# Layer 0 of a graph network in rounds of two pairs of batches (256 moving columns), with the mask's identity product taken from TensorE

## The chip, the cores and the metric

The kernel runs on one core of one Trainium2 chip. The metric is the device time of one execution in microseconds (us); a kernel is compared with the kernel before in rounds on the same chip. All times below are medians of several executions; a profile shows one execution, and its span is some 2 us shorter than the measured time.

## The reference

Four layers work on `x` (32 batches, 512 nodes, 128 features, float32) with one 512 x 512 matrix `adj`. Every layer adds a function of `h = relu(layernorm(x))` to `x`:

```python
# layer 0: an attention matrix A from the mask adj > 0 (the same for all batches)
m = adj > 0
vals = e[0][cumsum(m) - 1]
A = softmax(where(m, vals, NEG), axis=1)
x += (A * I) @ (h @ W[0]) + (A * (1 - I)) @ (h @ W[1]) + bias
# layer 1: hops with adj and its Chebyshev square, products with Theta, relu
# layer 2: weights = adj * adj; messages = weights^T @ relu(h @ psi); two small products
# layer 3: attention of h with itself, masked by adj
```

Layer 0 multiplies the same 512 x 512 matrix with the projected `h` of all batches. Layer 2 needs `adj` once more, in another order of its rows; the kernel reloads it (1 MB, called `sq`) and squares it at about 300 us.

## The kernel before

Batches go in pairs (16 of them). Layer 0 handles one pair in each round: a projection `g` of `h`, then seven half-size products instead of eight, each of 2 x 2 matmuls that move 128 columns, into three accumulators `a`, `c`, `d`, then terms for the diagonal.

```python
ORDER = ((1, "a", True), (6, "c", True), (5, "d", True), (7, "c", False), (2, "a", False),
         (4, "c", False), (3, "d", False))
def by_token(p, a, b, first):
    for i in range(2):
        for k in range(2):
            nc.tensor.matmul(p[:, i * D : (i + 1) * D], a[:, k, blk(i)], b[:, k, :], ...)
# [cut]
def project_steps(q, hT):
    g[q] = pair_tile(f"g_{q}")...            # five buffers of 2 x 512
    pg = [projected(f"p_g_{q}_{b}", (at(hT, b), w0[:, 1, :])) for b in range(2)]
```

`hT` is `h` with features on the partitions. From the fourth pair on it is made by VectorE (32 x 32 blocks) and a bounce through DRAM: four writes `d_hT` (128 KB each) and one read `hT` (512 KB), issued by SyncE, whose instructions follow one another in every trace here.

```python
d = bounce.tile(...)
for i in range(NQR):
    nc.sync.dma_start(d[:, :, i, :]..., hb[i * QR : (i + 1) * QR]...)
hT = feature_major(name)
nc.sync.dma_start(hT..., d...)
```

Square matrices share four buffers of 1 MB. `sq` is allocated in the code of layer 1, but its load is placed by a scheduler.

```python
def square_tile(name):
    return const.tile([P, NT, N], F32, tag="square", name=name, bufs=4)
# in the order of allocation: adj_s, cheb, att, attT, then sq (in att's place), adjTx, ...
def square():
    sq = square_tile("sq")
    load_crossed(sq, adj)                    # four transfers of 256 KB, by SyncE
    adjTx.append(square_tile("adjTx"))
    load_crossed(adjTx[0], adjT_d)
```

## Time and profile before

| | before |
|---|---|
| time, median of 3 (range) | 977.85 us (976.84 to 979.55) |
| span of the profile | 976.0 us |
| first product of layer 0 | 38.29 us |
| third pair's first product (the first two pairs done) | 63.89 us |
| first product of layer 1 | 200.2 us |
| layer 1's first product to the end | 775.8 us |

### The profile page before, as it was taken

What the parts mean: (1) busy time and instruction counts of PE and PEld (TensorE: products, weight loads), DVE (VectorE), ACT (ScalarE), POOL (GpSimd) and SP (SyncE); (2) the same over time, 40 slices, a digit from 0 to 9 for tenths busy, and PEclk for the clock granted to TensorE, in tenths of its full rate; (3) what the DMA queues carried; (4) which work ended last, traced back from release to release, by engine and by line L of the source; (5) the groups of instructions that cost most, each with busy time, mean ns of one, the idle gap of its engine ahead of it and who ended that gap; (6) DMA issues with size and microseconds to landing.
All of it is one profiled execution on the core that took longest, in us unless ns stands there. A gap on an engine that the chain in (4) does not pass through costs nothing.

```text
span 976.0 us, 16214 instructions
## 1 busy us (share of the span) xinstructions
PE 965.5 (99%) x5925; PEld 802.1 (82%) x5926; DVE 596.1 (61%) x1420; ACT 467.5 (48%) x1057; POOL 411.3 (42%) x519
## 2 busy tenths in 40 slices
PE   8999999999999999999999999999999999999998
PEld 4889999999999999999977777777667777777776
DVE  8788887755565655656576666556655444444444
ACT  3865445222322323238676644545674455444553
POOL 5779999841316313121244443344142332223322
PEclk9999999999999999999999999999999999999999
DMA  9255553522121221234343333332222121121111
GB/s 259 92 150 146 159 137 102 152 86 67 44 72 58 64 67 44 82 92 121 96 125 114 110 94 99 87 87 67 72 70 74 44 76 55 55 76 44 55 33 44
DMA packets 83056, 87.17 MB, mean 89 GB/s; under 512 B 6817, under 2 KB 73121, under 8 KB 82977
## 3 DMA queue, kind: packets, MB, share of 16 engines
q1 hardware_dynamic: 82976, 86.14, 31.1%
q8 instruction: 47, 0.77, 0.3%
q14 instruction: 33, 0.26, 0.1%
HBM read 44.70 MB, written 41.42 MB: 88 GB/s over the span
## 4 chain that ended last, share of the span: by engine, by line
PE 90%; DVE 3%; POOL 3%; ACT 1%; issue 1%; DMA 1%; DVEq 0%; POOLq 0%; ACTq 0%
PE p_av L887 12%; PE p_l L372 11%; PE p_score L872 11%; PE p_msgT_c L319 4%; PE p_x2T_c L319 4%; PE p_x1T_c L319 4%; PE p_l_c L326 4%; PE p_feat L372 3%; PE p_x1T_a L319 3%; PE p_hv L372 3%; PE p_x1T_d L319 3%; PE p_x2T_d L319 3%; PE p_x2T_a L319 3%; PE p_msgT_d L319 3%; PE p_msgT_a L319 3%; PE p_qkh L859 3%
## 5 line engine op out<-in xcount | busy, mean ns | idle before, releaser
L225 ACT ACTIVATE h<-x,sh,rs 128x128 f32<-128x128 f32 x448 | 182.5, 483 | 74.0 <-PE p_x2T_d L319 43.9
L877 POOL TENSOR_TENSOR ex<-ex,adjTx 128x512 f32<-128x512 f32 x64 | 83.4, 1305 | 206.3 <-ACT ex L875 201.7
L873 ACT ACTIVATE ex<-p_score 128x512 f32<-128x512 f32 x128 | 71.7, 588 | 122.7 <-issue 112.9
L887 PEld LDWEIGHTS p_av<-qkh_hv,ex 128*128 128x128 f32 x1024 | 118.4, 191 | 9.6 <-issue 7.2
L887 PE MATMUL p_av<-qkh_hv,ex 128*128 128x129 f32 x1024 | 120.3, 275 | 0.9 <-POOL ex L877 0.8
L872 PE MATMUL p_score<-qkh_hv,hT 128*128 128x512 f32 x256 | 115.2, 593 | 0.0
L259 DVE STREAM_TRANSPOSE hb_hT<-h 128x512 f32<-128x512 f32 x122 | 84.7, 699 | 21.0 <-ACT h L225 20.8
L877 DVE TENSOR_TENSOR ex<-ex,adjTx 128x512 f32<-128x512 f32 x64 | 46.0, 718 | 76.2 <-ACT ex L875 76.2
L872 PEld LDWEIGHTS p_score<-qkh_hv,hT 128*128 128x128 f32 x256 | 46.2, 190 | 46.5 <-issue 45.0
L197 DVE BATCH_NORM_STATS2 bn<-x 128x6 f32<-128x256 f32 x224 | 82.9, 418 | 1.3
L300 POOL TENSOR_TENSOR rt_h<-h 128x256 f32<-128x256 f32 x32 | 22.6, 728 | 133.4 <-PE p_x2T_c L319 133.1
L875 ACT ACTIVATE ex<-ex 128x512 f32<-128x512 f32 x128 | 76.6, 631 | 1.9
L300 POOL TENSOR_TENSOR rt_feat<-feat,feat 128x256 f32<-128x256 f32 x16 | 11.7, 729 | 126.7 <-ACT feat L828 126.7
L372 PE MATMUL p_l<-th,x2T 128*128 128x128 f32 x256 | 49.5, 275 | 0.0
L372 PE MATMUL p_l<-th,x1T 128*128 128x128 f32 x256 | 49.5, 275 | 0.0
L372 PE MATMUL p_l<-th,hs 128*128 128x128 f32 x256 | 49.5, 275 | 0.0
L372 PEld LDWEIGHTS p_hv<-vw,hT 128*128 128x128 f32 x256 | 33.6, 192 | 15.3 <-issue 8.1
L634 POOL COPY hs<-hT 128x512 f32<-128x512 f32 x32 | 19.6, 614 | 54.6 <-PE p_l L372 40.4
L636 POOL TENSOR_TENSOR hd<-hT,adiag 128x512 f32<-128x512 f32 x32 | 41.0, 1288 | 3.8 <-PE p_l_e L684 3.8
L209 ACT ACTIVATE sd<-bn,eps 128x8 f32<-128x8 f32 x60 | 17.9, 300 | 50.8 <-DVE bn L197 49.7
L345 ACT COPY x1T<-p_x1T_a 128x256 f32<-128x256 f32 x16 | 6.0, 372 | 74.1 <-PE p_x1T_a L319 74.1
L372 PEld LDWEIGHTS p_l<-th,hs 128*128 128x128 f32 x256 | 40.0, 192 | 0.8
(241 smaller groups left out, 2185.9 us busy)
## 6 DMA issues: line engine op xcount, KB each, us to landing
d_hT<-hb_hT SPq DMA_DIRECT2D x244, 128.0 KB, 2.4
hT<-d_hT SPq DMA_DIRECT2D x61, 512.0 KB, 3.6
x<-in_x_dram SPq DMA_DIRECT2D x28, 256.0 KB, 4.3
out_dram<-x SPq DMA_DIRECT2D x28, 256.0 KB, 2.3
adj_s<-in_adj_dram SPq DMA_DIRECT2D x4, 256.0 KB, 3.1
adjT_d<-adjT SPq DMA_DIRECT2D x1, 1024.0 KB
sq<-in_adj_dram SPq DMA_DIRECT2D x4, 256.0 KB
x_last<-in_x_dram SPq DMA_DIRECT2D x4, 256.0 KB
```

Of the source, the lines that this page charges most:

```text
L197: nc.vector.bn_stats(st[:, k].rearrange("p e s -> p (e s)"), xt[q][:, b, t : t + 2, :].rearrange("p t f -> p f t"))
L225: nc.scalar.activation(h[:, b, t, :], xt[q][:, b, t, :], AF.Relu, bias=shift[q][:, i : i + 1], scale=scale[q][:, i : i + 1])
L259: nc.vector.transpose(hb[:, :, b].rearrange("p j t r -> p t j r"), h[:, b].rearrange("p t (j c) -> p t j c", c=QR))
L319: nc.tensor.matmul(p[:, :H], b[:, k, :], a[:, k, :], start=(first and k == 0), stop=(k == 1), skip_group_check=True)
L326: nc.tensor.matmul(p[:, i * D : (i + 1) * D], a[:, k, blk(i)], b[:, k, :], start=(first and i == 0 and k == 0), stop=(k == 1), skip_group_ ...
L372: nc.tensor.matmul(p[:, blk(t)], hT(t), w, start=(i == 0), stop=(i == len(terms) - 1))
L636: nc.gpsimd.tensor_mul(split(s), src, split(scale))
L872: nc.tensor.matmul(ps, hT[:, t, b, :], qkh, start=True, stop=True)
L873: nc.scalar.activation(ex[:, t, :], ps, AF.Tanh, scale=1.0 / (8.0 * math.sqrt(D)))
L875: nc.scalar.activation(ex[:, t, :], ex[:, t, :], AF.Exp, scale=8.0)
L877: eng.tensor_mul(ex[:, t, :], ex[:, t, :], adjTx[0][:, t, :])
L887: nc.tensor.matmul(po[:, i, : D + 1], ex[:, t, blk(i0 + i)], hv[:, t, :], start=(t == 0), stop=(t == NT - 1))
```

## The change

The intent is to halve the number of matmuls in the products of layer 0 (two pairs share the stationary half of the attention matrix), and to take four matmuls with the identity off TensorE. A round now has two pairs, and `g` of such a round needs 1 MB. Buffers of 1 MB (`quad`, two of them) replace the pair buffers; where those don't suffice, every third `g` goes into a square buffer.

```diff
-        nc.tensor.matmul(p[:, i * D : (i + 1) * D], a[:, k, blk(i)], b[:, k, :],
+        nc.tensor.matmul(p[:, i * 2 * D : (i + 1) * 2 * D], a[:, k, blk(i)], b[:, k],
@@ [cut]
-    def pair_tile(name):
-        return work.tile([P, 2 * N + 2 * NT], F32, tag="pair", name=name, bufs=5)[:, : 2 * N]
+    def quad_tile(name):
+        return work.tile([P, 2, 2 * N + 2 * NT], F32, tag="quad", name=name, bufs=2)
@@
-        g[q] = pair_tile(f"g_{q}").rearrange("p (t b f) -> p t b f", t=NT, b=2)
+        r, w = divmod(q, 2)
+        if w == 0:
+            if r % 3 == 2:
+                g[r] = square_tile(f"g_{r}").rearrange("p t (b w f) -> p t b w f", b=2, w=2)
+            else:
+                t = quad_tile(f"g_{r}")...
@@ [cut: the start]
+    def entries(t):
+        nc.scalar.mul(us[t], m[:, t, :], elastn)
+        nc.gpsimd.tensor_add(att[:, t, :], us[t], att[:, t, :])
@@
-            nc.tensor.matmul(ph, at_row[:, kk, blk(t)], at_col[:, kk, :], start=(kk == 0), stop=False)
-        nc.tensor.matmul(ph, identh, m[:, t, :], start=False, stop=True)
+            nc.tensor.matmul(ph, at_row[:, kk, blk(t)], at_col[:, kk, :], start=(kk == 0), stop=(kk == NK - 1))
@@ [cut: rounds of two pairs, order of the start, buffers of layers 1 to 3]
```

## The prediction

> **What bounds the kernel now.** I read part 1 of the page first (which engine is full), then the chain of waits, then the windows of single rounds (what a round consists of), and last the timeline of the first 64 us, the only stretch where TensorE isn't simply full.
>
> ```profile
> PE 965.5 (99%) x5925; PEld 802.1 (82%) x5926; DVE 596.1 (61%) x1420; ACT 467.5 (48%) x1057; POOL 411.3 (42%) x519
> ```
>
> TensorE is busy 965.5 us of a span of 976.0; nothing else is above 82%. So the time is TensorE's queue of matmuls plus about 10 us in which it waits. Only two things can shorten the kernel: fewer or cheaper matmul cycles, or less of that waiting. The chain of waits shows where layers 0 and 1 lie and their periods:
>
> ```profile
> 113.43 1.79 PE p_g L372 x16
> 123.26 1.79 PE p_g L372 x16
> 133.08 1.79 PE p_g L372 x16
> ...
> 212.47 5.36 PE p_l L372 x48
> 229.91 5.36 PE p_l L372 x48
> ```
>
> Columns: start, duration, work, instructions. Layer 0 takes one pair of batches in 9.83 us (113.43 to 123.26), layer 1 in 17.44 us. A round of layer 0 is 56 product records (7 products, 4 matmuls each, every f32 matmul appearing as two records), 16 for the diagonal and 16 for p_g: 88 records in 9.825 us are 0.1117 us each, for 128 moving columns. The 48 p_l records say the same, 5.36 / 48 = 0.1117. Windows of one round of layer 0, and of the 56 product records of a layer-1 round (which move 256 columns):
>
> ```profile
> 113.43:123.26 9.83, 9.83 (x90) 9.83 (x90) 8.37 (x23) 4.76 (x12) 9.26 (x11) 1.00 0.57 163
> ...
> 217.83:229.91 12.08, 12.08 (x56) 10.28 (x55) 1.00 0.28 80
> ```
>
> In the first, PE, PEld, DVE, ACT and POOL follow the length: PE is full, GpSimd is busy 9.26 of 9.83, VectorE 8.37. In the second, 56 records of 256 columns take 12.08 us, 0.2157 each. So the width that this change brings is already measured inside this kernel. The start of layer 0 from the timeline:
>
> ```profile
> 25.30 0.70 ACT L563 ACTIVATE u<-u,least 128x512 f32<-128x512 f32 x1
> ...
> 33.87 1.04 PE L405 MATMUL p_attT<-ident,att 128*128 128x128 f32 x8
> ...
> 38.29 1.06 PE L326 MATMUL p_l_a<-g,attT 128*128 128x128 f32 x8
> ...
> 54.95 1.13 PE L326 MATMUL p_l_c<-rt_g,attT 128*128 128x128 f32 x8 [1.01 <-DVE u_l L696]
> ...
> 88.02 1.13 PE L326 MATMUL p_l_c<-rt_g,attT 128*128 128x128 f32 x8 [1.64 <-DVE u_l L696]
> ```
>
> Layer 0 starts at 38.29; layer 1's first product starts at 200.21 in the same view. The brackets are waits of TensorE for VectorE's eviction of an accumulator that is to be added to again.
>
> **What the Trainium skill says.** "TensorE: Matmul & The Clock Gate", section "Back-to-back issue gap", tabulates 134, 262 and 518 cycles for 128, 256 and 512 columns at 2.4 GHz: a fixed cost of about 6 cycles per matmul, whatever its width. Twice that (an f32 record behaves like two passes) is 111.7, 218.3 and 431.7 ns; the trace has 111.7, 215.7 and, for p_score (3.44 us for 8), 430. It agrees within 1.2%, and it says that doubling the width saves only the fixed cost, not half the time. The same section gives 81 ns for a sustained pair of weight load and 128-column matmul; no such floor shows above 111.7 ns here. "SBUF — State Buffer", section "SBUF: two separate sides", says that a VectorE instruction with two SBUF inputs and a GpSimd instruction lock one port pair against each other. The trace agrees in kind: the four sums of the attention matrix on VectorE took 742 ns for the first and 1107 to 1214 ns for those beside GpSimd's rt_g. "ScalarE: Activation LUTs", section "What ACT_TABLE_LOAD costs", gives 1283 ns and a drain of about 1380 ns; the trace has 1283 ns and the next instruction directly after it, so I count 1.28.
>
> **The change part by part.**
> (1) Products of layer 0: 16 x 56 = 896 records of 128 columns at 0.1117 become 448 of 256 at 0.2157. 100.1 us become 96.6: -3.4 us, all of it TensorE time in a stage that TensorE bounds. Diagonal and p_g records keep number and width. A round of two pairs is then 56 x 0.2157 + 64 x 0.1117 = 19.2 us where two rounds were 19.65.
> (2) The identity product on the mask: 4 matmuls of 512 bf16 columns leave (p_row, of the same form, takes 1.89 us for 8, so 0.24 each): 0.9 us of TensorE. But between 7.8 and 29.3 us VectorE runs with only one gap worth naming (0.90, before the reciprocal at 26.12) and feeds these matmuls, so I count nothing for it directly. In its place come 4 ScalarE multiplications (about 0.6 each, like the 589 ns of other 128x512 ones) and 4 GpSimd additions (1.29 each, like hd): 2.4 us and 5.2 us on engines that also make the first two normalised h. GpSimd's additions for rows 0 and 1 stand ahead of the first rs/sh chain: that chain ends at about 17.2 instead of 16.1. The second normalisation (8 x 0.40) is now wholly ahead of the first exponential, which I put at 26.8 instead of 25.30; the attention's last row leaves ScalarE at about 33.2 instead of 31.56.
> (3) Round 0 needs the projections of both first pairs. By the order of instructions, the last transposes of the attention matrix end at about 35.6 (34.9 before), and the attT copies wait on ScalarE for the square-root table (1.28) and on VectorE for g (2 x 0.69) and statistics (1.4). I get a first product at about 37.2, a little earlier than 38.29, because the Chebyshev matmuls that preceded it are moved into round 0. But after this product TensorE's queue has the transposes of pair 2, whose h ends on ScalarE at about 41: a wait of some 2.2 us. From 41.1 the rest of round 0 is 24.4 us of matmuls: 6 products 10.4, Chebyshev 6.9, diagonal 3.6, p_g 3.6. So round 1 starts at about 65.5. The kernel before had done the same work at 63.89: +1.6.
> (4) From there on, before: 136.3 us to 200.21, of which the work is 134.0 and waits are 2.3. After: 7 rounds of 19.24 less the 3.6 of p_g that the last lacks: 131.1 us, if nothing waits. That is -5.2.
> (5) VectorE: 16 evictions of 256 elements (425 ns) become 8 of 512 (about 0.69): 6.8 to 5.5 us per two pairs. GpSimd: eight rt of 0.75, six additions and two biases of 0.73 become 4 + 3 + 1 of 1.29: 11.8 to 10.3 us. Both get freer, off the path. Layers 1 to 3: the order of TensorE's instructions is the same apart from one swap of neighbours and the grouping of a few; the larger buffers keep the same depth (two pairs). I count 0.
> Sum: +1.6 - 5.2 = -3.6 us, to about 974.
>
> **The rivals.**
> Nothing but width and waits cancel: the longer start eats the gain (first exponential 2 to 3 us late, a longer wait for pair 2), giving 976 to 979. For it: the start is a chain through four engines, and two pairs now have to be ready. Against it: Chebyshev matmuls fill some of it.
> GpSimd becomes the bound of a round. For it: 9.26 of 9.83 us today, and it makes rt only after the projection of the second pair, 5.2 us of matmuls ahead of the product that needs it; ScalarE's copies take about 0.9 and two rt 2.6, so about 1.7 us are free. If sums of the adjacency matrix (1.28 each, two a round in four rounds) get in the way, each such round waits 1 to 2 us: 978 to 982. Against it: its work falls by 1.5 us per two pairs.
> The waits vanish and the start is no worse: then waits of about 4 us in layer 0 go too: about 969. For it: the accumulator that TensorE waited for at 54.95 and 88.02 was read 0.9 us of matmuls after it was written; now a product of 1.7 us, and mostly a projection of 1.8 us, stand between.
> Weight loads were the real limit of 128-column products (PEld is full in layer 0): then halving the loads would save far more. Against it: p_l in layer 1 runs at the same 0.1117 with PEld not full, and the 256-column rate is twice that within 3.5%.
>
> **Range and chances.** The sure part is -3.4; waits in layer 0 can add up to -4 more or give 4 back; the runs before spread over 2.7 us. I predict 973.8, with 969.5 to 978.0 for 8 in 10. Faster by 2% would need 958: there isn't that much waiting in the stage. Slower by 2% would need a wait of 3 us in each of the 8 new rounds.
>
> **What would show it.** The 448 products at 0.216 us each in a window of one round, and rounds of about 19.2 us from the second on (step 1, 4). The first exponential at 26 to 27.5 (step 2). The first product of layer 0 at 36 to 39 and a wait of TensorE just after it for the h of pair 2; the second round at 64 to 67 (step 3). The first product of layer 1 at about 196.6 instead of 200.21, and from there the same 776 us to the end (step 5). I am wrong if products take clearly less than 0.21, if rounds wait for rt or evictions, or if layers 1 to 3 change by more than 1 us.

## More of the kernel before

Columns: start, time until the issues were done, engine and line, what was transferred, number of issues.

```profile
35.06 2.74 SPq L99 DMA_DIRECT2D sq<-in_adj_dram  x4
...
160.61 1.76 SPq L264 DMA_DIRECT2D d_hT<-hb_hT  x4
...
164.48 0.34 SPq L267 DMA_DIRECT2D hT<-d_hT  x1
```

The reload of `adj` goes out at 35 us, in the start, between the loads of parameters and the first `hT`. In a round of layer 0 the read of `hT` follows its four writes by 3.9 us.

## The result, and the profile after

The changed kernel took 986.63 us (986.32 to 988.31, 6 executions), the kernel before 978.18 us (976.84 to 979.55) beside it. The ratio is 1.0088, 95% interval 1.0075 to 1.0101. (A ratio here is the mean time of one kernel's fast runs over that of the other's of the same rounds, so it is not quite the ratio of the medians.) So the kernel became slower by 0.9%, which counts as the same within 2%, but it lies outside the predicted range of 969.5 to 978.0.

The last two columns below belong to two experiments and are used later.

| us | before | changed | own buffers | own buffers, identity on TensorE |
|---|---|---|---|---|
| first exponential | 25.30 | 27.21 | 27.60 | 25.16 |
| second round of two pairs starts | 63.89 | 66.94 | 67.07 | 65.22 |
| first product of layer 1 | 200.2 | 209.0 | 199.1 | 197.2 |
| from there to the end | 775.8 | 775.6 | 775.6 | 775.8 |
| time, median | 978.2 | 986.63 | 976.54 | 974.58 |

Part 1 of the page of the changed kernel:

```profile
PE 965.6 (98%) x5473; PEld 788.0 (80%) x5474; DVE 597.3 (61%) x1363; ACT 469.6 (48%) x1059; POOL 402.7 (41%) x451
```

There are 452 matmul records fewer, as intended, but TensorE's busy time has not fallen at all. The table says where to look: layers 1 to 3 are unchanged, and everything is lost before layer 1. The chain of waits of the changed kernel in the last rounds of layer 0 (start, duration, work, instructions):

```profile
160.00 1.74 PE p_l_d L337 x8
161.83 0.71 SPq L99
...
163.95 10.68 DMA hT<-d_hT
...
174.76 3.76 PE p_g L385 x16
178.52 2.08 PE p_l_d L337 x8
```

Up to 163.4 the rounds take the predicted 19.24 us (the first of them 19.48). Then the chain leaves TensorE: three issues on SyncE's line 99 (the reload), one read of `hT` in flight for 10.68 us, and only then the projection `p_g` of pair 14. The projection itself takes 3.76 us, where it takes 1.79 before (shown in the prediction). TensorE waited 7.67 us for this `hT`. SyncE's queue of the changed kernel at this place:

```profile
157.57 1.75 SPq L269 DMA_DIRECT2D d_hT<-hb_hT  x4
161.83 1.88 SPq L99 DMA_DIRECT2D sq<-in_adj_dram  x3
163.95 0.39 SPq L272 DMA_DIRECT2D hT<-d_hT  x1
```

The reload, at 35 us before, now stands between the write and the read of an `hT` that TensorE wants at 167.1. The read goes out 2.4 us later than in the run with own buffers below (163.95 against 161.52), and its flight is some 7 us longer (10.68, against 3.4 in the median of this kernel). The reason is a buffer: the first free square buffer after the start is now taken by `g` of round 2 and then of round 5, and the load of `sq` has to wait for the last product of round 5 (the view of SyncE's waits has one of 2.4 us of line 99 for `p_l_d`). Windows of 2 us around the wait (length, then busy time and records of PE, PEld, DVE, ACT, POOL, granted clock, DMA share, GB/s):

```profile
172.00:174.00 2.00, 0.00 (x0) 0.00 (x0) 0.00 (x0) 0.00 (x0) 2.00 (x3) 0.57 0.48 143
...
176.00:178.00 2.00, 2.00 (x11) 2.00 (x11) 0.00 (x0) 0.58 (x1) 0.04 (x1) 0.50 0.40 89
...
180.00:182.00 2.00, 2.00 (x11) 1.76 (x10) 0.00 (x0) 0.00 (x0) 0.00 (x0) 1.00 0.06 14
```

The granted clock fell to half during the wait (at about 172) and came back only at about 179: this is why `p_g` and the `p_l_d` after it run long (3.76 + 2.08 for 1.79 + 1.73, 2.3 us). This also hides the wait in part 1: TensorE's busy time contains the slow records. "TensorE: Matmul & The Clock Gate" of the Trainium skill, section "What's actually happening", gives a clock of 4/8 after an idle window of about 3.4 us; the trace agrees, 0.50 after 7.67 us of idling, but a run below shows the same fall after shorter waits. Wait and slow clock make 10.0 us, which is the distance of 9.9 us between "changed" and "own buffers" in the table.

The second, smaller loss is in the start. The timeline of the changed kernel:

```profile
18.11 3.19 ACT L230 ACTIVATE h<-x,sh,rs 128x128 f32<-128x128 f32 x8 [2.93 <-POOL sh L212]
21.21 1.32 ACT L521 ACTIVATE u<-m,elastn 128x512 f32<-128x512 bf16 x2
...
24.11 3.19 ACT L230 ACTIVATE h<-x,sh,rs 128x128 f32<-128x128 f32 x8
27.21 0.71 ACT L594 ACTIVATE u<-u,least 128x512 f32<-128x512 f32 x1
...
42.49 1.97 PE L337 MATMUL p_l_c<-rt_g,sums_att 128*128 128x256 f32 x8 [0.81 <-DVE sums_att L290]
```

ScalarE works without a gap from 18.11 to the first exponential. It starts 2.0 us later than before (16.15), because GpSimd's chain for the first normalisation, with two of the new additions ahead of it, ends later, and two of the new multiplications (1.32 us) are among its work. The first exponential comes at 27.21, 1.9 us later than before (25.30), and the second round of two pairs starts 3.05 us later than the equal point before. (The six `at_part` on VectorE also slowed, from 2.17 to 4.08 us, beside two of GpSimd's additions. But VectorE had the first row's minimum ready at 26.19, so the exponential did not wait for them.)

### The profile page after: what moved, and what is told of

The parts are those of the page before. It is cut to its first block, busy times and chain, and to the rows that moved or that the text cites.

```text
span 984.6 us, 15193 instructions
## 1 busy us (share of the span) xinstructions
PE 965.6 (98%) x5473; PEld 788.0 (80%) x5474; DVE 597.3 (61%) x1363; ACT 469.6 (48%) x1059; POOL 402.7 (41%) x451
## 4 chain that ended last, share of the span: by engine, by line
PE 93%; DVE 3%; DMA 2%; ACT 1%; issue 0%; SPq 0%; POOL 0%; DVEq 0%; ACTq 0%
PE p_av L944 12%; PE p_l L385 11%; PE p_score L929 11%; PE p_msgT_c L330 4%; PE p_x2T_c L330 4%; PE p_x1T_c L330 4%; PE p_l_c L337 4%; PE p_feat L385 3%; PE p_msgT_d L330 3%; PE p_x1T_a L330 3%; PE p_msgT_a L330 3%; PE p_hv L385 3%; PE p_x2T_d L330 3%; PE p_x1T_d L330 3%; PE p_x2T_a L330 3%; PE p_phi L899 3%
## 5 line engine op out<-in xcount | busy, mean ns | idle before, releaser
L230 ACT ACTIVATE h<-x,sh,rs 128x128 f32<-128x128 f32 x512 | 208.6, 483 | 91.5 <-PE p_x2T_d L330 46.9
L202 DVE BATCH_NORM_STATS2 bn<-x 128x6 f32<-128x256 f32 x256 | 93.0, 418 | 1.6
L385 PE MATMUL p_l<-th,x12T 128*128 128x128 f32 x512 | 78.1, 275 | 0.0
L385 PEld LDWEIGHTS p_l<-th,x12T 128*128 128x128 f32 x512 | 67.5, 192 | 0.0
L894 POOL TENSOR_TENSOR x<-x,phi2b 128x256 f32<-128x256 f32 x64 | 44.9, 732 | 0.0
L358 ACT COPY x12T<-p_x1T_a 128x256 f32<-128x256 f32 x16 | 6.0, 372 | 74.4 <-PE p_x1T_a L330 74.4
```

What stands on the lines that cost most here:

```text
L202: nc.vector.bn_stats(st[:, k].rearrange("p e s -> p (e s)"), xt[q][:, b, t : t + 2, :].rearrange("p t f -> p f t"))
L230: nc.scalar.activation(h[:, b, t, :], xt[q][:, b, t, :], AF.Relu, bias=shift[q][:, i : i + 1], scale=scale[q][:, i : i + 1])
L385: nc.tensor.matmul(p[:, blk(t)], hT(t), w, start=(i == 0), stop=(i == len(terms) - 1))
L894: tc.keep_in_program_order(nc.gpsimd.tensor_add(xi, xi, spread(phi2b, 2)))
```

## The experiments

Theory: the reload of `adj`, moved by a square buffer from the start into layer 0, delays an `hT` past TensorE's slack, and this costs the 10 us. Rivals: rounds of two pairs are too tight for their `hT` whatever else is transferred; the start is to blame; the wider matmuls bring nothing. Each run was compared with the kernel before in its own rounds (976.8 to 979.8 us there). They ran on three chips, but the median of the kernel before was 978.1 to 978.2 on each, so they can be set side by side.

**Buffers of its own for every g.** Only the condition changes; the result stays right, as in all runs below.

```diff
-            if r % 3 == 2:
+            if False:
```

> The projections g of all eight pairs of pairs go into buffers of their own, none into a square one, so the reload of the adjacency matrix (sq) goes out in the start again, at about 36 us, as before the change. Reload theory: the round of pairs 12 to 15 falls from 29.3 us to 19.2, the 7.67 us wait for hT goes, the granted clock stays at 1.0 there, layer 1's first product comes at about 199 us and the time is about 976.5. Rival 'two-pair rounds are too tight for the transfers of hT': the wait stays, time 985 to 987. Rival 'the start is to blame': nothing changes, 986.

Measured: 976.54 us (976.01 to 976.7), ratio 0.9977 (0.9962 to 0.9992). SyncE's queue, then the projection of pair 14 in TensorE's timeline:

```profile
157.70 1.75 SPq L269 DMA_DIRECT2D d_hT<-hb_hT  x4
161.52 0.34 SPq L272 DMA_DIRECT2D hT<-d_hT  x1
```
```profile
167.06 1.95 PE L385 MATMUL p_g<-w,hT 128*128 128x128 f32 x16
```

Nothing stands between write and read, `p_g` starts without a bracket (no wait), and its clock is full. The rounds of two pairs are thus not too tight by themselves, and the start (67.07, like the changed kernel's 66.94) is not what makes the kernel slower than the one before.

**The reload pinned to layer 1.** Buffers as in the changed kernel; the four transfers are kept behind what precedes them in the program.

```diff
-            nc.sync.dma_start(dst[:, b, :], src.rearrange(...)[b])
+            load = nc.sync.dma_start(dst[:, b, :], src.rearrange(...)[b])
+            if pin:
+                tc.keep_in_program_order(load)
@@
-        load_crossed(sq, adj)
+        load_crossed(sq, adj, pin=True)
```

> Buffers as in the changed kernel (two of the g still in square buffers), only the four transfers of the reload are held back by program order until layer 1, about 300 us. Reload theory (the transfer's place, not the buffer, is what costs): same as with buffers of their own, about 976.5, layer 1's first product at about 199. If the square buffers themselves cost something (a wait for one of them), this stays above the run with buffers of their own by that much. Rivals: 985 to 987.

Measured: 977.0 us (975.62 to 977.61), ratio 0.9981 (0.9966 to 0.9996). So it is the place of the transfers and not the square buffer itself. (The profile has two waits that the others lack, 0.63 us for `u_l` at 154.9 and 1.43 us for `rt_g` at 166.3. Why is not shown; the changed kernel has the same buffers and doesn't have them.) SyncE's queue in layer 1 of this run:

```profile
255.62 2.81 SPq L99 DMA_DIRECT2D sq<-in_adj_dram  x4
258.80 10.23 SPq L99 DMA_DIRECT2D adjTx<-adjT_d  x4
269.14 4.22 SPq L271 DMA_DIRECT2D d_hT<-hb_hT  x4
281.44 0.34 SPq L274 DMA_DIRECT2D hT<-d_hT  x1
```

The same kind of delay is there: behind both reloads, `hT` is read 12.3 us after its writes are issued, not 3.8. But the timeline has no wait of TensorE between 255 and 300 us. Layer 1 takes 17.4 us for one pair (shown in the prediction) and asks for each `hT` early enough.

**Only the first g in a square buffer.** The reload then goes out three rounds earlier.

```diff
-            if r % 3 == 2:
+            if r == 2:
```

> Only the first of the two g (pairs 4 and 5) stays in a square buffer, so the reload goes out about two thirds through the round of pairs 4 and 5, ahead of the read of pair 8's hT, with loads of x behind it. Reload theory in its strong form (any reload of 1 MB amid layer 0 delays the next hT beyond its slack): a wait of TensorE of 5 to 9 us for one hT in the third or fourth round, lower granted clock after it, 983 to 987. Weak form (it needs the queue blocked at just the wrong place): no wait, 976 to 978.

Measured: 988.26 us (986.87 to 988.47), ratio 1.0093 (1.0076 to 1.011). SyncE's queue, and TensorE at this place:

```profile
104.29 1.88 SPq L99 DMA_DIRECT2D sq<-in_adj_dram  x3
106.41 0.84 SPq L272 DMA_DIRECT2D hT<-d_hT  x1
```
```profile
118.90 3.75 PE L385 MATMUL p_g<-w,hT 128*128 128x128 f32 x16 [9.46 <-DMA hT<-d_hT]
```

The loss follows the reload to another round (a wait of 9.46 us at 118.9 and none at 174). The strong form of the theory held, a little above its range.

**The turning of the pair after next asked for two products earlier.** This was meant to put `hT` ahead of the reload.

```diff
+            elif i == 2:
+                if A + 4 < NQ:
+                    go(turn(A + 4))
@@
-            elif i == 4:
-                if A + 4 < NQ:
-                    go(turn(A + 4))
```

> Buffers and reload as in the changed kernel; only the transposition of the pair after next is asked for two products earlier in each round (some 3.5 us), so its write and read of hT stand ahead of the reload in the queue of transfers. Reload theory by blocking in the queue: hT is no longer behind the reload, the wait of 7.67 us falls to 0 to 2 us, time 976 to 979. If bandwidth shared with the reload and not the order in the queue is what costs: hT takes as long as in the changed kernel (about 10 us), and the wait only falls by the 3.5 us, time about 983. Rivals: 985 to 987.

Measured: 994.14 us (990.84 to 996.33), ratio 1.0155 (1.0132 to 1.0179): outside all expectations. SyncE's queue in an early round, and TensorE there:

```profile
71.27 7.82 SPq L269 DMA_DIRECT2D d_hT<-hb_hT  x6
79.31 0.34 SPq L272 DMA_DIRECT2D hT<-d_hT  x1
```
```profile
83.55 2.02 PE L385 MATMUL p_g<-w,hT 128*128 128x128 f32 x16 [1.76 <-DMA hT<-d_hT]
...
127.36 3.31 PE L385 MATMUL p_g<-w,hT 128*128 128x128 f32 x16 [1.91 <-DMA hT<-d_hT]
```

The scheduler now put two of the four writes of the next pair ahead of the read of this one. Those two wait for VectorE's transposes, and the read behind them goes out at 79.31, 8 us after its first write. TensorE waits for an `hT` six times before layer 1, 1.25 to 2.86 us each and 11.5 us in all. The reload itself goes out at 177.05, behind pair 14's `hT`. The run therefore doesn't separate what it was made for, but it shows the queue at work without any reload: what waits at its head delays what stands behind it. It also shows that the length of a wait alone doesn't decide on the clock: after waits of 1.84, 1.91 and 2.86 us it fell to 0.50 (16 records of `p_g` in 3.16 to 3.31 us), after 1.25, 1.76 and 1.90 it stayed at full (2.02).

**The reload just behind pair 14's hT.** Buffers as in the changed kernel; the load is pinned to the beginning of round 6.

```diff
@@ [cut: pin, as in the run with the reload pinned to layer 1]
             if i == 0:
+                if r == 6:
+                    early.append(square_tile("sq"))
+                    load_crossed(early[0], adj, pin=True)
                 if C + 2 < NQ:
                     go(turn(C + 2))
@@ [cut: square() takes early[0]]
```

> Buffers as in the changed kernel, and the reload of 1 MB stays in layer 0; only its four transfers are put just behind the read of pair 14's hT in the one queue, not ahead of it. If the place in the in-order queue is what costs: pair 14's hT lands some 3.5 us after its issue, TensorE waits for it 0 us instead of 7.67, and the next write of d_hT is the one that is held up, with some 10 us to spare: 976.5 to 979. If it is the bytes in this stage, wherever they stand: a wait of 4 to 8 us remains, at pair 14's or pair 15's hT, 981 to 986.

Measured: 981.52 us in the median of three executions, ratio 1.0036 (1.002 to 1.0051). One of its four executions, the profiled one, took 1689.59 us at a granted clock of 0.56; it is slow and was left out.

> The kernel of the run with the reload behind pair 14's hT once more, because its profiled execution was a throttled one (clock 0.56) and can't be compared. It took 982 us, 5.4 more than without the reload in layer 0, where 0 to 2.5 had been expected. If the transfers are served in the order of the queue: pair 14's hT lands in about 3.5 us and TensorE doesn't wait for it, but the four writes of pair 15's d_hT, issued at about 167 us, land some 7 us late behind 1 MB, and TensorE waits 3 to 5 us for pair 15's hT at about 177 us. If bandwidth is merely shared: a wait at pair 14's hT too.

Measured: 982.78 us (2 executions). SyncE's queue and TensorE:

```profile
161.75 2.64 SPq L99 DMA_DIRECT2D sq<-in_adj_dram  x4
167.14 3.95 SPq L271 DMA_DIRECT2D d_hT<-hb_hT  x6
177.14 0.34 SPq L274 DMA_DIRECT2D hT<-d_hT  x1
```
```profile
181.05 3.75 PE L387 MATMUL p_g<-w,hT 128*128 128x128 f32 x16 [3.55 <-DMA hT<-d_hT]
```

(The edit shifts line numbers by two here.) Pair 14's `hT`, issued at 161.20, is now in time: its `p_g` starts at 166.86 without a wait. The delay has moved on to pair 15: its four writes are issued at 167.14 but its read only at 177.14 (172.94 with own buffers), and TensorE waits 3.55 us and pays the slow clock again (3.75 us, where this view has 1.95 at full clock). So the place in the queue decides which transfer is late. It doesn't remove the lateness; the second expectation, "the bytes in this stage, wherever they stand", came nearer than "0 to 2.5 us".

**One piece instead of three ahead of pair 14's hT.** The other three are pinned to layer 1.

```diff
-        for b in range(NQR):
-            nc.sync.dma_start(...)
+        for b in reversed(range(NQR)):
+            load = nc.sync.dma_start(...)
+            if b >= free:
+                tc.keep_in_program_order(load)
@@
-        load_crossed(sq, adj)
+        load_crossed(sq, adj, free=1)
```

> As the changed kernel, but one of the four transfers of the reload (256 KB) stays ahead of pair 14's hT, where there were three; the other three go out in layer 1. In the changed kernel three of them (with the wait for the buffer) brought hT 7.3 us more of flight and 2.6 us of later issue. With one: issue some 1.2 us late, flight 1.7 to 2.4 us longer, against some 3 us of slack: TensorE waits 0 to 2 us, time 976.5 to 979. If any reload there costs the whole wait (a stall that doesn't grow with the bytes): 984 to 987.

Measured: 979.67 us (978.76 to 980.66), ratio 1.0017 (1.0003 to 1.0031), 3.1 us above own buffers and 0.7 us above the range. TensorE's timeline at pair 14's projection:

```profile
169.52 2.02 PE L387 MATMUL p_g<-w,hT 128*128 128x128 f32 x16 [2.06 <-DVE bn L204]
```

The wait is 2.06 us, and the clock stays at full (16 records in 2.02 us). The profile names a VectorE instruction as what ended it. With own buffers the same projection started before that instruction, so it can't be what is needed, and `hT`, read from 163.10 on, is the only other thing that is different. It is read so and not shown by a line. The loss grows with the bytes ahead of `hT`: 3.1 us for one piece and 10.1 for three, about in proportion as far as two points can say.

**The kernel before with a late reload.** One `g` of the kernel before goes into a square buffer, so that three pieces of the reload stand ahead of pair 14's `hT` there too.

```diff
-        g[q] = pair_tile(f"g_{q}").rearrange("p (t b f) -> p t b f", t=NT, b=2)
+        if q == 11:
+            gq = square_tile(f"g_{q}").rearrange("p t e -> p (t e)")[:, : 2 * N]
+        else:
+            gq = pair_tile(f"g_{q}")
+        g[q] = gq.rearrange("p (t b f) -> p t b f", t=NT, b=2)
```

> The kernel before, with the projection of pair 11 in a square buffer, so that the reload goes out ahead of pair 14's hT there too. Rounds of one pair fetch hT more than a round (9.8 us) ahead of its use. If the stall needs the changed kernel's rounds of two pairs, in which hT is used some 6 us after its issue: no wait of TensorE, 977 to 980. If the reload in layer 0 alone is enough: a wait of 5 to 8 us, 983 to 988.

Measured: 985.11 us (983.94 to 986.04), ratio 1.0076 (1.006 to 1.0091). SyncE's queue and TensorE:

```profile
162.42 1.88 SPq L99 DMA_DIRECT2D sq<-in_adj_dram  x3
164.47 1.11 SPq L267 DMA_DIRECT2D hT<-d_hT  x1
```
```profile
176.74 3.12 PE L372 MATMUL p_g<-w,hT 128*128 128x128 f32 x16 [4.42 <-DMA hT<-d_hT]
```

Here the reload doesn't delay the issue of `hT` (164.47, against 164.48 without it); only its flight is longer, some 12 us, where 3.6 is the median. The kernel before pays 7 us for the same misplaced reload. So rounds of two pairs are not the condition; they only leave less slack (the wait is 7.67 us there and 4.42 here).

**The reload in a queue of its own.** The same place as behind pair 14's `hT`, but issued by ScalarE.

```diff
-            load = nc.sync.dma_start(dst[:, b, :], ...)
+            load = (nc.scalar if pin else nc.sync).dma_start(dst[:, b, :], ...)
@@ [cut: the rest as in the run with the reload behind pair 14's hT]
```

> The same place in the program as the reload behind pair 14's hT, but its four transfers are issued by ScalarE, so in a queue of their own. If the delay comes from standing behind 1 MB in one queue: pair 15's hT gets about half of the bandwidth at once, its write and read take 1.5 to 2 times as long for some 10 us, TensorE waits 0 to 2 us, 976.5 to 979. If the delay is the engines' bandwidth, whoever's queue: as with one queue, about 982.

Measured: 982.78 us (981.93 to 984.45), ratio 1.0051 (1.0037 to 1.0065), as with one queue. TensorE's timeline:

```profile
182.37 3.75 PE L387 MATMUL p_g<-w,hT 128*128 128x128 f32 x16 [4.13 <-DMA hT<-d_hT]
```

The wait at pair 15's `hT` is 4.13 us. "DMA: Bandwidth & Descriptors", section "Rules for kernel authors", says that spreading DMAs over the issuing engines doesn't help, because they run on the same 16 DMA engines and interleave there. This run agrees: the reload costs the same from either queue.

**Width alone.** Own buffers, and each product's matmul of 256 columns split again into two of 128.

```diff
-                nc.tensor.matmul(p[:, i * 2 * D : (i + 1) * 2 * D], a[:, k, blk(i)], b[:, k], ...)
+                for w in range(2):
+                    nc.tensor.matmul(p[:, (2 * i + w) * D : (2 * i + w + 1) * D], a[:, k, blk(i)], b[:, k, w, :], ...)
```

> The kernel with buffers of its own for every g, and each product's matmul of 256 columns split again into two of 128: 896 records of 0.1117 us for 448 of 0.2157 are 3.4 us more of TensorE in rounds that TensorE bounds: about 980.0 against 976.5, rounds of 19.7 instead of 19.24 us. If the width brings nothing: 976.5. If the weight loads of 128-column products were what bounds (twice as many loads): more than 985.

Measured: 981.01 us (979.91 to 981.31), ratio 1.0027 (1.0015 to 1.004), 4.5 us above own buffers where 3.4 were expected. The start of two rounds in TensorE's timeline:

```profile
87.71 1.95 PE L338 MATMUL p_l_a<-g,attT 128*128 128x128 f32 x16
...
107.37 1.95 PE L338 MATMUL p_l_a<-g,attT 128*128 128x128 f32 x16
```

A round takes 19.66 us, the predicted 19.7, against 19.24. The gain of the width is real and as small as computed, and weight loads were not the limit (more than 985 us would have shown that). The remaining microsecond is not in the period of the rounds: in the last round TensorE waits 1.36 us for VectorE, where it waits 0.36 with own buffers.

**The identity product back on TensorE.** Own buffers, and the start's new multiplications and additions replaced by the old matmul.

```diff
@@ [cut: own buffers, the identity tile]
-        nc.scalar.mul(us[t], m[:, t, :], elastn)
-        nc.gpsimd.tensor_add(att[:, t, :], us[t], att[:, t, :])
+        pass
@@
-            ... start=(kk == 0), stop=(kk == NK - 1))
+            ... start=(kk == 0), stop=False)
+        nc.tensor.matmul(ph, identh, m[:, t, :], start=False, stop=True)
```

> Buffers of its own for every g, and the identity product on the mask back on TensorE (no multiplications on ScalarE, no additions on GpSimd in the start). The start of the changed kernel ran about 1.9 us behind the kernel before at the first exponential and 3.2 us at the equal point of layer 0. If the replacement is what delays it: first exponential at about 25.5 us, second round at 65 to 66 instead of 67.1, time 974.5 to 975.5 against 976.5. If two pairs to be made ready are what delays it: 976.5 as before.

Measured: 974.58 us (974.14 to 977.12), ratio 0.997 (0.9956 to 0.9984). The intervals of this run and of own buffers overlap (0.9962 to 0.9992), so the times alone don't separate them. The traces do. ScalarE's timeline and TensorE's:

```profile
25.16 0.72 ACT L596 ACTIVATE u<-u,least 128x512 f32<-128x512 f32 x1
```
```profile
65.22 1.89 PE L339 MATMUL p_l_a<-g,attT 128*128 128x256 f32 x8
```

The first exponential is at 25.16 instead of 27.60, the second round at 65.22 instead of 67.07, layer 1 at 197.2 instead of 199.1. These are single profiles, and the start itself comes earlier or later from run to run (the first record of `p_row`, the first product of the mask, between 10.02 and 11.59). Counted from that record the second round starts after 55.7 us with own buffers, 53.6 with the identity back and 53.1 in the kernel before. The replacement of the identity product thus costs some 2 us, and some 0.5 us of delay stay with the second pair. This is the version that beats both kernels: 12 us below the changed kernel and 3.5 us below the one before (clear of the noise, but within the 2% that count as the same).

## Why the prediction was wrong

**Step 1, the width:** right. 8 records take 1.73 us, 0.216 each; a round takes 19.24 us; split again it takes 19.66.

**Step 2, the identity product:** right in kind, and a loss as said, but undersized. The first exponential came at 27.21 (predicted 26.8). ScalarE sets it, and its first normalised `h` waited for GpSimd's `rs`/`sh` chain, which ended at 18.08, where the prediction had said 17.2. With the identity product back on TensorE some 2 us are undone at the second round.

**Step 3, the start of the rounds:** +1.6 was predicted, +3.05 measured. The first product came at 37.44 (predicted 37.2), and from the second product to the second round it was 24.45 us (predicted 24.4). The miss lies between them: the second product started at 42.49 instead of 41.1. The transposes of pair 2 ended at 41.7, and then TensorE waited 0.81 us for VectorE's first two sums of the attention matrix, which took 1.80 and 1.64 us (0.74 and 1.11 before). The prediction quoted the shared port pair for just these sums, but its step 3 has no term for them. (Its reading "742 ns for the first and 1107 to 1214 ns for those beside GpSimd's rt_g" is not quite right: the first sum, at 36.12, also runs beside `rt_g`, which works from 35.58 on.)

**Step 4, "131.1 us, if nothing waits":** this is where it fell, together with the sentence in step 5 (said there of layers 1 to 3) that "the larger buffers keep the same depth". The 131.1 itself was nearly right: 132.0 from the second round to layer 1 with own buffers, 132.0 with the identity product back. But the clause "if nothing waits" was not examined for transfers. Depth was counted per kind of buffer; that a `g` in a square buffer occupies the place from which the reload of `adj` started at 35 us was overlooked. None of the four rivals concerned a transfer. (The sum had already taken out the 2.3 us of waits of the kernel before; the range and the rival "the waits vanish" take out some 4 us again, and so count them in part twice.) The runs put 10 us on it: 7.67 us of waiting and 2.3 us at half clock, removed when the buffer is changed (own buffers) or when only the transfers are moved (layer 1).

**Step 5, layers 1 to 3 unchanged:** right, 775.6 against 775.8.

With the failed step repaired the rest of the sum stands: own buffers gave 976.54, 2.7 above the predicted 973.8; with the identity product back on TensorE it is 974.58. What stays open is how the DMA engines share their time between the reload and the transfers behind it. In the changed kernel the engines were busy 92 and 96% of the windows 166 to 168 and 168 to 170 us, but only 31% of 164 to 166 and 43% of the last 2.6 us before `hT` arrived, so it is not a plain lack of bandwidth. At 167.22 SyncE also issued six of the `d_hT` writes that follow (128 KB each), which share the engines with the late `hT`; no run here says how much of the flight is theirs.

## What to carry to other kernels

When a change gives a tile to another pool, ask who took that buffer next before, and when: a load that starts "as soon as a buffer is free" moves with it, here from an idle stretch into a stage where it cost 10 us. Look at the queue of the issuing engine, not only at the compute engines, and put a large transfer that nobody needs soon into a stage with slack, here layer 1, where the same delay of `hT` cost nothing. A wait of TensorE can cost more than itself, because the clock may fall: here it did after each wait of 2.86 us and more, and after two of 1.84 and 1.91, and that added 1.7 to 3.0 us.

## What the Trainium skill lacked or had wrong

- "DMA: Bandwidth & Descriptors" says that issuing engines are not separate DMA queues, which the runs confirm (982.78 us from either queue). No number there tells what a transfer pays behind others: a read of 512 KB took 3.4 to 3.6 us in the median, 10.68 us behind three pieces of 256 KB in the changed kernel, and some 12 us in the kernel before.
- The same page gives no cost for the other half of the delay, an instruction in SyncE's queue that waits for a buffer or for data and holds what stands behind it: the read of `hT` went out 2.4 us later behind the reload (163.95 against 161.52), and 8 us after its first write behind two writes of the next pair.
- "TensorE: Matmul & The Clock Gate" gives an idle window of about 3.4 us for the fall to 4/8. The 0.50 is right, after waits of 3.55, 4.42 and 7.67 us for one, but it also came after waits of 1.84 and 1.91 us, and not after 1.90 and 2.06. What it added to a wait in a full stage was 1.7 to 3.0 us here.
- The same page gives 81 and 131 ns for sustained pairs of weight load and matmul at 128 and 512 columns; this kernel never showed those: an f32 record of 128 columns took 111.7 ns (of 256 columns 216), and bf16 matmuls of 512 columns 215 ns (6 in 1.29 us).
- "SBUF — State Buffer" explains the shared port pair as an exclusive lock; the runs give its size on whole stretches: six `at_part` on VectorE took 2.16 and 2.17 us without GpSimd's additions beside them, and 3.11 to 4.27 with them. A sum went from 0.74 to 1.80 us; GpSimd's `rt_g` stood beside both, twice as wide in the second.
- "ScalarE: Activation LUTs" gives about 1380 ns of drain with a table load; no drain was seen: the load at 34.57 of the changed kernel follows the instruction before it at once, and the next one follows its 1.28 us at once.
